# Layer 2 of a graph network: gathered rows in buffers of four, run rows stored in pairs side by side

## Chip, cores and metric

One core of one Trainium2 chip. The time is device microseconds of one execution; the kernel before was run three times.

## What is computed

Four graph layers (mean, max-pool, gcn, mean) over 6250 nodes and 100,000 edges, sorted by destination, and a last product. The change is in the aggregation of layer 2, a maximum over the incoming edges:

```python
def _sage_pool(h, src, dst, n, deg, W_pool, b_pool, W_self, W_neigh, b):
    hp = jax.nn.relu(h @ W_pool + b_pool)
    hmax = jax.ops.segment_max(hp[src], dst, num_segments=n)
    hmax = jnp.where(deg[:, None] > 0, hmax, 0.0)
    return h @ W_self + hmax @ W_neigh + b
```

`hp` has 6250 rows of 512 float32, 2 KB each.

## The kernel before

Everything runs in one program; a framework turns the Python below into instruction streams per engine, orders them, and adds semaphore waits where tiles depend on each other. A tile of a pool with `bufs=n` takes the place of the one made n tiles earlier and waits for its last readers; a pool opened on the memory of a closed one waits for the last readers there.

**Layer 1** gathers rows of `tab_h` (L483), sums them with matrix products and writes `hp` to `tab_p`, the first part of the DRAM tensor `rows2` (L1162). Beside it `segments()` (L596) finds for each edge whether it has the same destination as the one before it in its lane (`same`), and row numbers for a later fix (`fixI`).

**Layer 2's maximum** (L1566 to L1633) works on the edges in six blocks of `BLOCKS = (52, 100, 220, 180, 130, 100)` steps, last block first. In a block of `tb` steps, lane p of the 128 partitions holds `tb` consecutive edges, and step t takes the t-th edge of every lane: one indirect DMA on GpSimd gathers 128 rows of `tab_p` into `X` (L1574), and VectorE folds them into `run`, the maximum since the current destination began (`step`, L1555). Since a node's maximum stands where its last edge was, the running rows must be kept in DRAM, but only one for each pair of steps: the row after the odd step t is made so that it also holds what ended at t-1 (L1589). So each pair has two operations on `run` and one on `X[:, 0, :]`, and one store of that row to the block's part of `rows2`:

```python
        def stored(b, r0, rows):
            n = rows.shape[1]
            nc.sync.dma_start(
                runs[b][r0 * P : (r0 + n) * P, :].rearrange("(g p) f -> p g f", p=P), rows)
```

`X` holds two steps; its six buffers alternate between two pools, `xpool` (three buffers, also scratch memory in layer 1) and `xmore` (three). Row g of lane p lies at `g * P + p` of the block's rows. The last pair of a block stores both rows of `X` at once.

Around the steps, generators are advanced step by step: `products2` (L1326) multiplies the weights together on TensorE and forms the bias rows, and ends with adds to `qrow` (L288, L1352); at step 64 (`MADE_AT`) what is left of it is issued and its pool `fw2` is closed, and the pool `early3` opened on its memory. `finding` (`node_rows`, L1179) computes for every block and node the row in `rows2` that holds its maximum; its first seven pieces come before the steps, the others one every 12 steps from step 130. `build_narrow` makes adjacency tiles with one-hot operands (`hm`, L374). After a block, `carry` (L1358) passes maxima from lane to lane, gathers one row for each lane (`fixf`, L1383) and stores the mended ones; then `done2` (L1459) gathers for each tile of 128 nodes a row from each block it lies in (`tot`, L1450), takes their maximum, multiplies, and writes `tab_r`, which layer 3 gathers. `early_products` begins layer 3's products. All gathers are issued by GpSimd in the order of its stream; stores of `X` are issued by SyncE.

Of the kernel before, what the change touches and what calls it, by code (L numbers as in the profile page):

```python
# [20 lines left out]
P = 128  # L21
# [56 lines left out]
def fast_path(  # L78
# [90 lines left out]


    assert all(tb % 2 == 0 for tb in BLOCKS)
    kept = [tb // 2 + 1 for tb in BLOCKS]

    n_of = [n * P + 1 + P for n in kept]
    run_at = [NP + sum(n_of[b + 1 :]) for b in range(NB)]
# [397 lines left out]
    G2 = 2  # L573
    upto2 = ctx.enter_context(ExitStack())
    ahead = upto2.enter_context(tc.tile_pool(name="ahead", bufs=1, side="right"))
    xpool = upto2.enter_context(tc.tile_pool(name="xrows", bufs=3, side="right"))
    srcI = ahead.tile([P, T], I32, name="srcIf")
    same = ahead.tile([P, T], F32, name="samef")
    fixI = ahead.tile([P, NB], I32, name="fixIf")
# [8 lines left out]
    def kept_row(b, t, whole, half):  # L588

        nc.vector.tensor_copy(whole, t)  # L590
        nc.vector.tensor_single_scalar(whole, whole, 1, op=ALU.logical_shift_right)
        nc.vector.tensor_copy(half, whole)
        nc.vector.tensor_scalar(t, t, -(BLOCKS[b] / 2.0 - 1.0), None, op0=ALU.add)
        nc.vector.tensor_tensor(t, t, half, op=ALU.max)

    def segments():  # L596
        dstI, dstF, eqf = scratch(T, I32), scratch(T), scratch(T)
        flen, fhalf = (ahead.tile([P, 1], F32, name=n) for n in ("flenf", "fhalf"))
        flenI = ahead.tile([P, 1], I32, name="flenI")
        for b, tb in enumerate(BLOCKS):  # L600
            t0 = offs[b] // P
            for flat, put in ((sflat, srcI), (dflat, dstI)):
                tc.keep_in_program_order(nc.sync.dma_start(
                    put[:, t0 : t0 + tb],
                    flat[offs[b] : offs[b + 1]].rearrange("(p t) -> p t", t=tb),
                ))
        for _ in range(60):
            yield 1
        nc.vector.tensor_copy(dstF, dstI)
        nc.vector.tensor_tensor(same[:, 1:], dstF[:, 1:], dstF[:, : T - 1], op=ALU.is_equal)  # L610
        yield 1
        for b, tb in enumerate(BLOCKS):
            t0 = offs[b] // P
            sl_ = slice(t0, t0 + tb)
            nc.vector.memset(same[:, t0 : t0 + 1], 0.0)
            nc.vector.tensor_copy(rows_df[:, b : b + 1], dstF[:, t0 : t0 + 1])
            nc.vector.tensor_copy(rows_dl[:, b : b + 1], dstF[:, t0 + tb - 1 : t0 + tb])
            nc.vector.tensor_scalar(eqf[:, sl_], dstF[:, sl_], rows_df[:, b : b + 1], None,
                                    op0=ALU.is_equal)
            nc.vector.tensor_reduce(flen, eqf[:, sl_], AX.X, ALU.add)  # L620
            nc.vector.tensor_scalar(flen, flen, -1.0, None, op0=ALU.add)
            kept_row(b, flen, flenI, fhalf)
            nc.vector.tensor_scalar(flen, flen, float(P), float(run_at[b]), op0=ALU.mult,
                                    op1=ALU.add)
            nc.vector.tensor_add(fixI[:, b : b + 1], flen, pidx)
            yield 1


# [455 lines left out]
    with ExitStack() as on:  # L1084
# [86 lines left out]
        for d in range(H1):  # L1171
# [2 lines left out]
        sums(wk, psg, tab_h, FI, srcT, keyT, JC * P, H1, done1, 14, hub, counts=3, todo=todo, rest=24,  # L1174
             aside=[own_ahead(), tail_checks(wk), segments()])
    layer1.close()


    def node_rows(pool, psm):  # L1179
# [28 lines left out]
        for b, tb in reversed(list(enumerate(BLOCKS))):  # L1208
            z = float(run_at[b] + kept[b] * P)
            nc.vector.tensor_scalar(q, end, float(offs[b + 1]), -1.0 - offs[b], op0=ALU.min,  # L1210
                                    op1=ALU.add)
            nc.vector.scalar_tensor_tensor(ok, q, 0.0, has, op0=ALU.is_ge, op1=ALU.mult)
            nc.vector.scalar_tensor_tensor(ok, beg, float(offs[b + 1]), ok, op0=ALU.is_lt,
                                           op1=ALU.mult)
            nc.vector.tensor_mul(q, q, ok)
            yield
            nc.vector.tensor_scalar(pI, q, 1.0 / tb, None, op0=ALU.mult)
            nc.vector.tensor_copy(pF, pI)
            nc.vector.scalar_tensor_tensor(t_, pF, -float(tb), q, op0=ALU.mult, op1=ALU.add)
            nc.vector.tensor_scalar(off, t_, 0.0, None, op0=ALU.is_lt)  # L1220
            nc.vector.tensor_sub(pF, pF, off)
            nc.vector.scalar_tensor_tensor(t_, off, float(tb), t_, op0=ALU.mult, op1=ALU.add)
            yield
            nc.vector.tensor_scalar(off, t_, float(tb), None, op0=ALU.is_ge)
            nc.vector.tensor_add(pF, pF, off)
            nc.vector.scalar_tensor_tensor(t_, off, -float(tb), t_, op0=ALU.mult, op1=ALU.add)
            yield
            kept_row(b, t_, pI, off)
            nc.vector.scalar_tensor_tensor(t_, t_, float(P), pF, op0=ALU.mult, op1=ALU.add)

            yield
            nc.vector.scalar_tensor_tensor(off, pF, float(tb), beg, op0=ALU.mult,
                                           op1=ALU.subtract)
            nc.vector.tensor_scalar(off, off, -float(offs[b]), None, op0=ALU.is_ge)
            if b:
                nc.vector.tensor_scalar(pF, pF, float(kept[b] * P + 1), None, op0=ALU.add)
                nc.vector.tensor_sub(pF, pF, t_)
                nc.vector.tensor_mul(pF, pF, off)
                nc.vector.tensor_add(t_, t_, pF)
            else:  # L1240
                nc.vector.tensor_mul(off, off, ok)
                nc.vector.tensor_scalar(pF, pF, 1.0, None, op0=ALU.add)
                nc.vector.tensor_mul(pF, pF, off)
                nc.vector.tensor_scalar(pF, pF, -1.0, None, op0=ALU.add)
                for d in last_tiles:
                    lanes = bank(psm, "pm", "lanes", (P,))
                    nc.tensor.transpose(lanes, pF[:, d : d + 1].to_broadcast([P, P]), ident)
                    yield
                    takes[d] = pool.tile([P, P], F32, name=f"takes{d}", bufs=1)
                    nc.vector.tensor_scalar(takes[d], lanes, pidx, None, op0=ALU.is_equal)  # L1250
            yield
            nc.vector.tensor_scalar(t_, t_, float(run_at[b]), None, op0=ALU.add)
            nc.vector.tensor_sub(off, only, t_)
            nc.vector.tensor_mul(off, off, lone)
            nc.vector.tensor_add(t_, t_, off)
            nc.vector.tensor_scalar(t_, t_, -z, None, op0=ALU.add)
            nc.vector.tensor_mul(t_, t_, ok)
            nc.vector.tensor_scalar(rows_of[b], t_, z, None, op0=ALU.add)
            yield
# [31 lines left out]
    with tc.tile_pool(name="fl2c", bufs=1) as ck, ExitStack() as late:  # L1291
# [11 lines left out]
        nc.scalar.dma_start(mkR, stash_k[:, 1, RB1:])  # L1303
        keepT = ck.tile([P, NB, P], F32, name="keepTf")
        contT = ck.tile([P, NB, P], F32, name="contTf")
        xmore = late.enter_context(tc.tile_pool(name="xrows2", bufs=3))

        def chains():

# [244 lines left out]
        def step(put, held, st, row):  # L1554
            nc.vector.scalar_tensor_tensor(put, held, st, row, op0=ALU.mult, op1=ALU.max)  # L1555

        def stored(b, r0, rows):
            n = rows.shape[1]
            nc.sync.dma_start(
                runs[b][r0 * P : (r0 + n) * P, :].rearrange("(g p) f -> p g f", p=P), rows)  # L1560

        tiles, begun2, begun_at = [], 0, 0
        ends = []
# [2 lines left out]
        for b in reversed(range(NB)):  # L1566
            tb = BLOCKS[b]
            t0 = offs[b] // P
            run = psr.tile([P, FH], F32, name="run")
            for s0 in range(0, tb, G2):  # L1570
                X = (xmore if at // G2 % 2 else xpool).tile([P, G2, FH], F32, name="X2")
                for k in range(G2):
                    t = t0 + s0 + k
                    nc.gpsimd.indirect_dma_start(  # L1574
                        out=X[:, k, :], out_offset=None, in_=tab_p,
                        in_offset=bass.IndirectOffsetOnAxis(ap=srcI[:, t : t + 1], axis=0),
                    )
                    row, st = X[:, k, :], same[:, t : t + 1]
                    if s0 + G2 >= tb:
                        step(row, X[:, 0, :] if k else run, st, row)  # L1580
                        if k:
                            stored(b, s0 // 2, X)
                    elif k == 0 and s0:
                        step(run, run, st, row)
                    elif k:
                        held = run if s0 else X[:, 0, :]
                        if s0 == 0:
                            step(run, held, st, row)
                        step(X[:, 0, :], row, st, held)  # L1589
                        if s0:  # L1590
                            step(run, run, st, row)
                        stored(b, s0 // 2, X[:, :1, :])
                    at += 1
                    if at > 8:
                        next(steps, None)
# [4 lines left out]
                    if at == MADE_AT:  # L1600
                        for _ in steps:
                            pass
                        top.close()
                        early_pool.append(
                            top.enter_context(tc.tile_pool(name="early3", bufs=1)))
                    if at <= EARLY_AT:
                        hub.advance(math.ceil(len(first) * max(0, at - 16) / (EARLY_AT - 16)))
                    else:
# [18 lines left out]
                    for g in list(now):  # L1627
                        if next(g, 0) == 0:
                            now.remove(g)
            end = carry(b, X[:, 1, :])  # L1630
            next(end)
            ends.append(end)
            last_b = b  # L1633
# [784 lines left out]
```

## Time and profile before

| | |
|---|---|
| median of 3 runs | 2730.45 us (2728.73 to 2737.01) |
| the profiled execution | 2726.43 us |
| its span on the core | 2724.6 us |
| granted TensorE clock, mean | 0.944 |
| busy shares of the span | PE 87%, VectorE 76%, GpSimd 71%, ScalarE 33% |
| DMA | 805.91 MB, mean 296 GB/s |
| gathers of X (L1574) | 782, 742.5 us busy |
| steps on VectorE (L1555) into run, into X | 758, 571.0 us; 379, 281.4 us |
| stores of X (SyncE) | 385 of 256 KB, 6 of 512 KB |

The profile shows one execution. A group's line gives its source line, engine and operation, the tiles written and read, the count, the busy time and mean duration, and the idle time of the engine just before, with what ended it. A row of stretches gives start and end, length, busy time with count for each engine, then the granted clock, the mean share in which the 16 DMA engines were busy, and GB/s. A row of the timeline gives start, length, engine, line and operation, and in brackets the idle time before it and its releaser. A row of the chain gives start, length and what the chain that ended last went through.

### The profile page before, as it was taken

How to read it: one execution, taken by the hardware profiler on the slowest of the kernel's cores; microseconds unless marked ns; L12 is line 12 of the kernel's file. 1: busy time of each engine (PE TensorE's matmuls, PEld its weight loads, DVE VectorE, ACT ScalarE, POOL GpSimd, SP SyncE). 2: the span in 40 equal slices, each digit the busy share in tenths (PEclk: the TensorE clock that was granted, in tenths of full speed). 3: DMA queues.
4: the chain of work that ended last, by engine and by line, in shares of the span. 5: the costliest groups of instructions: out<-in, count | busy, mean ns of one | idle time of the engine just before them, and what ended most of it. 6: DMA issues, size and time to landing. Idle time of an engine off the chain costs nothing.

```text
span 2724.6 us, 39212 instructions
## 1 busy us (share of the span) xinstructions
PE 2368.6 (87%) x11542; PEld 1282.5 (47%) x11674; DVE 2076.7 (76%) x5555; ACT 904.5 (33%) x2190; POOL 1938.3 (71%) x2266
## 2 busy tenths in 40 slices
PE   4698999999786675989899939986999999999998
PEld 2356667677443332434344414442444444565554
DVE  8898777766699798889789988972767766466665
ACT  5567767764388777212111111110000101000000
POOL 6477777777577777777677777745777775677776
PEclk8799999999897887999899969998999999999999
DMA  9467677777799999999999999979999998888886
GB/s 288 150 185 206 206 211 216 217 230 221 245 377 354 337 362 362 345 359 352 312 351 356 348 336 344 348 243 351 379 378 393 386 363 309 248 239 240 238 247 200
DMA packets 352251, 805.91 MB, mean 296 GB/s; under 512 B 56174, under 2 KB 150870, under 8 KB 351996
## 3 DMA queue, kind: packets, MB, share of 16 engines
q0 software_dynamic: 146080, 513.79, 57.3%
q1 hardware_dynamic: 139368, 206.78, 20.9%
q10 hardware_dynamic: 66580, 82.73, 8.9%
q8 instruction: 95, 1.56, 0.2%
q14 instruction: 128, 1.05, 0.1%
HBM read 604.99 MB, written 198.91 MB: 295 GB/s over the span
## 4 chain that ended last, share of the span: by engine, by line
PE 47%; DMA 28%; DVE 12%; issue 6%; POOL 3%; ACT 1%; ACTq 0%; SPq 0%; DVEq 0%; another core or an unknown queue 0%; POOLq 0%
PE pd L564 12%; PE pg L505 11%; DMA X<-rows,srcIf 11%; DVE run L1555 5%; PE pd L556 4%; DMA rows<-X 4%; DMA ring<-tab_h,srcT 4%; PE pm_hp L1157 3%; DVE X L1555 3%; DMA ring<-tab_s,srcE 2%; PE pd L557 2%; POOL X L1574 2%; PE pm_hp L1154 2%; PE pb L346 2%; PE pg L500 2%
## 5 line engine op out<-in xcount | busy, mean ns | idle before, releaser
L1574 POOL DMA_INDIRECT X<-rows,srcIf x782 | 742.5, 950 | 276.3 <-issue 146.4
L1555 DVE SCALAR_TENSOR_TENSOR run<-run,samef,X 128x512 f32<-128x512 f32 x758 | 571.0, 753 | 42.3 <-DMA X<-rows,srcIf 37.1
L483 POOL DMA_INDIRECT ring<-tab_h,srcT x474 | 456.3, 963 | 148.9 <-issue 56.4
L505 PE MATMUL pg<-ring,hot 128*128 128x259 bf16 (+1 forms) x2432 | 512.1, 320 | 53.2 <-DMA ring<-tab_h,srcT 30.7
L534 DVE SCALAR_TENSOR_TENSOR acc<-pg,M,acc 128x256 f32<-128x256 f32 (+2 forms) x694 | 356.3, 538 | 106.0 <-PE pg L505 76.8
L483 POOL DMA_INDIRECT ring<-tab_r,srcE x342 | 331.7, 970 | 133.5 <-issue 54.9
L564 PE MATMUL pd<-r,ae 128*128 128x512 bf16 x1492 | 372.6, 385 | 32.9 <-DVE acc L1286 30.3
L483 POOL DMA_INDIRECT ring<-tab_s,srcE x314 | 299.4, 954 | 117.5 <-PE pg L501 38.6
L505 PEld LDWEIGHTS <-hot 128*128 128x128 bf16 x2448 | 239.6, 98 | 257.8 <-issue 98.3
L1555 DVE SCALAR_TENSOR_TENSOR X<-X,samef,run 128x512 f32<-128x512 f32 x379 | 281.4, 742 | 43.0 <-DMA X<-rows,srcIf 13.1
L556 PE MATMUL pd<-zt,ac 128*128 128x512 bf16 x835 | 291.0, 382 | 7.1 <-DMA ac<-tab_a 5.5
L564 PEld LDWEIGHTS <-ae 128*128 128x128 fp8e4 x1536 | 151.6, 99 | 250.3 <-issue 110.1
L479 DVE TENSOR_SCALAR hot<-iota_bf,keyE 128x128 bf16<-128x128 bf16 x656 | 159.3, 267 | 115.1 <-PE pg L505 82.0
L557 PE MATMUL pd<-zt,ac 128*128 128x256 bf16 x882 | 241.6, 274 | 2.7 <-DVE zt L312 0.2
L564 PE MATMUL pd<-zt,ac 128*128 128x512 bf16 x797 | 221.8, 380 | 0.9
L1482 PE MATMUL pm_prf<-unf,hTf 128*128 128x512 f32 x384 | 187.8, 615 | 5.6 <-ACT hTf L1472 5.4
L564 PE MATMUL pd<-Z,A 128*128 128x256 bf16 (+1 forms) x1176 | 184.4, 274 | 0.7 <-ACT A L351 0.6
L338 ACT ACTIVATE hs<-ht,onef 128x128 bf16<-128x128 bf16 x396 | 153.4, 393 | 90.2 <-PE pb L346 88.6
L346 PE MATMUL pb<-hm,hs 128*128 128x392 bf16 x461 | 146.3, 337 | 11.7 <-DVE hm L340 11.5
L337 ACT ACTIVATE ht<-iota_bf,sk 128x128 bf16<-128x128 bf16 x396 | 153.0, 398 | 8.3
L340 DVE TENSOR_SCALAR hm<-iota_w,mk 128x392 bf16<-128x392 f16 x461 | 149.7, 332 | 5.2 <-PE pb L346 4.7
L479 DVE TENSOR_SCALAR hot<-iota_bf,keyT 128x128 bf16<-128x128 bf16 x474 | 122.5, 267 | 40.6 <-PE pg L505 39.4
(381 smaller groups left out, 3498.9 us busy)
## 6 DMA issues: line engine op xcount, KB each, us to landing
rows<-X SPq DMA_DIRECT2D x385, 256.0 KB
tab_r<-r ACTq DMA_DIRECT2D x49, 384.0 KB
rows<-hpf SPq DMA_DIRECT2D x49, 256.0 KB
th<-tab_t ACTq DMA_DIRECT2D x49, 256.0 KB
X<-rows,srcIf POOLq DMA_INDIRECT x782
ac<-tab_a ACTq DMA_DIRECT2D x90, 112.0 KB
tab_t<-th SPq DMA_DIRECT2D x37, 256.0 KB
tab_h<-Z SPq DMA_DIRECT2D x16, 579.0 KB
```

What stands on the lines that cost most here:

```text
L338: nc.scalar.activation(hots[0], t, AF.Relu, bias=one, scale=-1.0)
L346: nc.tensor.matmul(hold[0], hots[0], hots[1], start=(k == 0), stop=(k == k_of[w] - 1))
L479: nc.vector.tensor_scalar(hot[j], iota_b, keyT[:, j - jb : j - jb + 1], None, op0=ALU.is_equal)
L483: nc.gpsimd.indirect_dma_start(out=ring[:, j % deep, :], out_offset=None, in_=table, in_offset=bass.IndirectOffsetOnAxis(ap=srcT[:, j - jb ...
L505: nc.tensor.matmul(pg[:, : F + c], hot[j], X[:, part * F : (part + 1) * F + c], start=(k == 0 and part == 2), stop=(k == n - 1 and part == 1),
L534: nc.vector.scalar_tensor_tensor(acc[d], half, m, acc[d], op0=ALU.mult, op1=ALU.add)
L556: nc.tensor.matmul(hold[0], a, z[:, : 2 * F], start=(s == ss[0]), stop=False)
L557: nc.tensor.matmul(hold[0][:, :F], a, z[:, 2 * F :], start=False, stop=(s == ss[-1]))
L564: nc.tensor.matmul(hold[0][:, : F + c], a, z[:, part * F : (part + 1) * F + c], start=(s == ss[0] and part == 2 and s != own), stop=(s == ...
L1482: nc.tensor.matmul(pm, hT[:, c, :], un[:, c, :], start=False, stop=(c == KH - 1))
L1555: nc.vector.scalar_tensor_tensor(put, held, st, row, op0=ALU.mult, op1=ALU.max)
L1574: nc.gpsimd.indirect_dma_start(out=X[:, k, :], out_offset=None, in_=tab_p, in_offset=bass.IndirectOffsetOnAxis(ap=srcI[:, t : t + 1], axis=0),
```

## The change

`X` now holds four steps. Its buffers come in turn from `xrows2` (two) and `xrows3` (one), and from step 64 on also from `xrows4` (one), which is opened after `early3` on the memory that `fw2` left. The run row of the first pair goes to `X[:, 0, :]`, that of the second to `X[:, 1, :]`, and both leave in one store after the fourth step. In DRAM the two lie side by side for each lane: row g of lane p is at `(g // 2) * 2 * P + 2 * p + g % 2`, and `kept` rounds the rows of a block up to even. `twin` turns a row g into `g + (g // 2) * (2 * P - 2)` for the row numbers in `segments` and `node_rows`. The last buffer of a block is stored whole, two or four rows. `xpool` is closed after layer 1.

```diff
-    kept = [tb // 2 + 1 for tb in BLOCKS]
+    kept = [(tb // 2 + 2) // 2 * 2 for tb in BLOCKS]
...
+    def twin(t, whole, half):
+
+        nc.vector.tensor_copy(whole, t)
+        nc.vector.tensor_single_scalar(whole, whole, 1, op=ALU.logical_shift_right)
+        nc.vector.tensor_copy(half, whole)
+        nc.vector.scalar_tensor_tensor(t, half, float(2 * P - 2), t, op0=ALU.mult, op1=ALU.add)
...
             kept_row(b, flen, flenI, fhalf)
-            nc.vector.tensor_scalar(flen, flen, float(P), float(run_at[b]), op0=ALU.mult,
-                                    op1=ALU.add)
-            nc.vector.tensor_add(fixI[:, b : b + 1], flen, pidx)
+            twin(flen, flenI, fhalf)
+            nc.vector.tensor_scalar(flen, flen, float(run_at[b]), None, op0=ALU.add)
+            nc.vector.scalar_tensor_tensor(fixI[:, b : b + 1], pidx, 2.0, flen, op0=ALU.mult,
+                                           op1=ALU.add)
...
             kept_row(b, t_, pI, off)
-            nc.vector.scalar_tensor_tensor(t_, t_, float(P), pF, op0=ALU.mult, op1=ALU.add)
+            twin(t_, pI, off)
+            nc.vector.scalar_tensor_tensor(t_, pF, 2.0, t_, op0=ALU.mult, op1=ALU.add)
...
-        xmore = late.enter_context(tc.tile_pool(name="xrows2", bufs=3))
+        xpools = [upto2.enter_context(tc.tile_pool(name="xrows2", bufs=2, side="right")),
+                  late.enter_context(tc.tile_pool(name="xrows3", bufs=1))]
+        xpools.append(xpools[0])
...
-        def stored(b, r0, rows):
+        def stored(b, h, rows):
             n = rows.shape[1]
             nc.sync.dma_start(
-                runs[b][r0 * P : (r0 + n) * P, :].rearrange("(g p) f -> p g f", p=P), rows)
+                runs[b][2 * h * P : (2 * h + n) * P, :].rearrange("(g p t) f -> p g (t f)", p=P, t=2),
+                rows.rearrange("p (g t) f -> p g (t f)", t=2))
...
-            for s0 in range(0, tb, G2):
-                X = (xmore if at // G2 % 2 else xpool).tile([P, G2, FH], F32, name="X2")
-                for k in range(G2):
+            for s0 in range(0, tb, 4):
+                n = min(4, tb - s0)
+                X = xpools[0].tile([P, 4, FH], F32, name="X4")
+                xpools.append(xpools.pop(0))
+                for k in range(n):
...
-                    if s0 + G2 >= tb:
-                        step(row, X[:, 0, :] if k else run, st, row)
-                        if k:
-                            stored(b, s0 // 2, X)
-                    elif k == 0 and s0:
+                    put = X[:, k // 2, :]
+                    if s0 + k >= tb - 2:
+                        if k % 2 == 0:
+                            step(put, run, st, row)
+                        else:
+                            last = X[:, k // 2 + 1, :]
+                            step(last, put, st, row)
+                            stored(b, s0 // 4, X[:, :n, :])
+                    elif k % 2 == 0 and s0 + k:
                         step(run, run, st, row)
-                    elif k:
-                        held = run if s0 else X[:, 0, :]
-                        if s0 == 0:
+                    elif k % 2:
+                        held = run if s0 + k > 1 else X[:, 0, :]
+                        if s0 + k == 1:
                             step(run, held, st, row)
-                        step(X[:, 0, :], row, st, held)
-                        if s0:
+                        step(put, row, st, held)
+                        if s0 + k > 1:
                             step(run, run, st, row)
-                        stored(b, s0 // 2, X[:, :1, :])
+                        if k == 3:
+                            stored(b, s0 // 4, X[:, :2, :])
...
                         early_pool.append(
                             top.enter_context(tc.tile_pool(name="early3", bufs=1)))
+                        xpools.append(top.enter_context(tc.tile_pool(name="xrows4", bufs=1)))
```

More of the change, by code (lines that the diff above doesn't have):

```diff
@@ L575, in fast_path @@
     ahead = upto2.enter_context(tc.tile_pool(name="ahead", bufs=1, side="right"))
-    xpool = upto2.enter_context(tc.tile_pool(name="xrows", bufs=3, side="right"))
+    upto1 = ctx.enter_context(ExitStack())
+    xpool = upto1.enter_context(tc.tile_pool(name="xrows", bufs=3, side="right"))
     srcI = ahead.tile([P, T], I32, name="srcIf")
@@ L1176, in fast_path @@
     layer1.close()
+    upto1.close()
     def node_rows(pool, psm):
@@ L1629, in fast_path @@
                             now.remove(g)
-            end = carry(b, X[:, 1, :])
+            end = carry(b, last)
             next(end)
```

## Prediction

> **What bounds the kernel now.** The change touches layer 2 alone, so I read that stage first by stretches, then GpSimd's order of time in it, then its groups, the DMA queues and the chain. Layer 2 runs from the first gather (721 us) to the last store (1824 us):
>
> ```profile
> core 0: us, PE busy (x) PEld busy (x) DVE busy (x) ACT busy (x) POOL busy (x), PEclk, DMA share, GB/s
> 721.00:1824.00 1103.00, 904.79 (x3259) 429.82 (x3305) 975.97 (x1904) 412.43 (x897) 800.24 (x844) 0.90 0.98 346
> ```
>
> The tempting reading is the DMA share of 0.98: the stage looks bound by its transfers, which this change makes cheaper. GpSimd looks idle for a quarter of the stage. Its timeline says otherwise:
>
> ```profile
> 842.51 0.95 POOL L1574 DMA_INDIRECT X<-rows,srcIf  x1 [0.30 <-issue]
> 843.76 0.95 POOL L1574 DMA_INDIRECT X<-rows,srcIf  x1 [0.30 <-issue]
> 845.01 0.95 POOL L1574 DMA_INDIRECT X<-rows,srcIf  x1 [0.30 <-DMA rows<-X]
> 846.26 0.95 POOL L1574 DMA_INDIRECT X<-rows,srcIf  x1 [0.30 <-issue]
> ```
>
> Gathers start every 1.25 us: 0.95 busy and 0.30 that no wait explains, the same 0.30 whether a releaser is named or not. Is that period GpSimd's own, or does a full DMA hold it back? The gathers of layer 1 (first row below) answer: 462 in 586 us is 1.27 each at a DMA share of 0.71. So 1.25 us is GpSimd's own cost of an indirect DMA.
>
> ```profile
> 104.00:690.00 586.00, 444.98 (x462) 0.98 0.71 209
> 721.40:821.80 100.40, 72.13 (x76) 0.92 0.99 362
> 821.80:842.40 20.60, 15.12 (x16) 1.00 1.02 388
> 842.40:865.10 22.70, 15.38 (x16) 0.82 0.97 323
> 865.10:1815.30 950.20, 639.05 (x674) 0.90 0.98 345
> ```
>
> ```profile
> L1574 POOL DMA_INDIRECT X<-rows,srcIf x782 | 742.5, 950 | 276.3 <-issue 146.4 <-DVE run L1555 35.5 <-DVE X L1555 25.6
> L1450 POOL DMA_INDIRECT tot<-rows,rows_of x55 | 52.0, 946 | 16.8 <-issue 10.4 <-DMA rows<-X 2.1 <-DMA X<-rows,srcIf 1.5
> L1383 POOL DMA_INDIRECT fixf<-rows,fixIf x5 | 4.7, 944 | 1.5 <-issue 0.9 <-DVE cTf L1373 0.3 <-DVE segf L1369 0.3
> L1555 DVE SCALAR_TENSOR_TENSOR X<-X,samef,run 128x512 f32<-128x512 f32 x379 | 281.4, 742 | 43.0 <-DMA X<-rows,srcIf 13.1 <-issue 12.9 <-DVE hm L374 7.0
> ```
>
> 843 indirect DMAs (782, 55, 5 and one more total) by 1.25 are 1054 us of the 1094 from 721.4 to 1815.3. All real waiting of GpSimd is the other 40: 6 in the first 92 steps (121.0 less 115), 2.7 in the next 16, and 31.5 behind (950.2 less 735 by 1.25). The number of gathers doesn't change. So the change can win at most these waits, and every microsecond by which it holds GpSimd back is never caught up.
>
> **The change part by part.**
>
> *Fewer, larger stores.* The built program has 196 stores of X instead of 391, nearly all with 4 KB side by side per lane.
>
> ```profile
> q0 software_dynamic: 67440, 221.04, 58.9%
> q1 hardware_dynamic: 75952, 113.28, 27.7%
> q10 hardware_dynamic: 21504, 46.32, 11.3%
> rows<-X SPq DMA_DIRECT2D x385, 256.0 KB
> ```
>
> q1 carries them: 27.7% of 1103 us is 306 us for 113 MB, 2.7 us a MB at 1.5 KB a packet; q10 pays 2.7 at 2.2 KB, so packet size matters little. Between nothing and 5% of the stores' 104 MB gives 0 to 14 us of 16-engine time. GpSimd paces the stage, so I take 0 on the path, bounds -14 and 0. SyncE loses 195 issues it had time for: 0. The Trainium skill, "DMA: Bandwidth & Descriptors", section "Rules for kernel authors", says to coalesce many small transfers into one large one; by it this part gains, and it is a rival below. The same page, section "Anatomy of one DMA", has a DMA cost about 2.0 us plus its bytes at 436 GB/s, an estimate of 0.6 us later landing for 512 KB than for 256 KB, which speaks against it where someone waits for the landing.
>
> *Three buffers of four, until step 64.* A buffer is filled again when its store has landed. The chain prices gathers and stores under load:
>
> ```profile
> 783.77 6.28 DMA X<-rows,srcIf
> 790.90 5.88 DMA rows<-X
> 860.62 5.50 DMA rows<-X
> 870.15 5.10 DMA X<-rows,srcIf
> ```
>
> So a gather takes about 5.7 us until its step can run, a store 5.7 until GpSimd goes on. Before, a buffer's round is 1.25 (two issues) + 5.7 + 1.1 (DVE for the last row) + 5.7 = 13.8 us (the 1.1 is the 0.74 of its operation, L1555 above, and some waiting), and six buffers of two give GpSimd 12 by 1.25 = 15.0: 1.2 to spare. Now the fourth issue comes 3.75 after the first: 16.3 us against the same 15.0. The ring binds: 15 us for the first 12 steps and 64 by 1.36 for the rest of the first 76 are 102 us, beside 100.4 measured. If all the early hiccups (about 5) add to that and stores land 0.7 later (5 rounds, 4 us), it is +11; if they vanish in the ring, +2. I take +6.
>
> *The fourth buffer.* xrows4 is opened after step 64 on the memory of fw2, the pool of the weight products. I read the built order and its waits: the first gather into it (steps 76 to 79) waits for the last reader there, the add of b4r to qrow, and GpSimd gets the gathers of steps 80 to 91 ahead of it. DVE has no step to do between step 75 and that gather. In its order there now stand 145 instructions between step 75's last and the add of qrow: 13 hm, three adds of the bias rows, and 129 small ones, the row numbers of node_rows pulled forward.
>
> ```profile
> 847.27 3.60 PE L282 MATMUL pm_b<-B4f,col 128*128 128x512 f32 x8
> 851.77 0.60 DVE qrowf L288
> 852.55 0.33 DVE qrowf L1352
> 827.99 0.75 DVE L1555 SCALAR_TENSOR_TENSOR run<-run,samef,X 128x512 f32<-128x512 f32 x1
> 736.94 0.18 DVE L1224 TENSOR_SCALAR nr<-nr 128x49 f32<-128x49 f32 x1
> 737.21 0.20 DVE L1225 TENSOR_TENSOR nr<-nr,nr 128x49 f32<-128x49 f32 x1
> 737.33 0.20 DVE L1226 SCALAR_TENSOR_TENSOR nr<-nr,nr 128x49 f32<-128x49 f32 x1
> L374 DVE TENSOR_SCALAR hm<-iota_w,mkR 128x196 bf16<-128x196 f16 x320 | 87.5, 284 | 0.9 <-PE pb L390 0.8
> ```
>
> The 827.99 row is step 75's last operation, ending 828.7; with the +6 it ends at 834.7. Small operations follow each other at 0.27 us where one needs the last (736.94 to 737.21), 0.12 where not. At 0.20 they take 26 us (15 to 35), hm 3.7, the adds 1.8: the add of qrow ends at 866 (855 to 875). TensorE's products put it at 853 at the earliest, as now. So the gather of step 76 starts at 866, where it started at 821.8. Queued behind it on GpSimd is every later gather, the carries' and totals' too; DVE waits for its rows.
>
> Steps 92 to 95 need that same buffer once more: 3.75 + 5.7 + 1.1 + 5.5 = 16 after 866, so 882, where before they began at 842.4: **+40 us** (+27 if qrow is at 853).
>
> *Afterwards, four buffers.* 16 rows give 20 us against a round of 16.3: 3.7 to spare, where there were 1.2. A hiccup of DVE that costs GpSimd something now costs up to 2.5 less, and the row numbers are already out of DVE's way. Of the 31.5 us of later waiting I give back 11; bounds 4 (they come in clusters at the ends of blocks, where one allowance serves several) and 25.
>
> *Row numbers, twin.* A net of four tiny DVE operations a block in layer 1 and in node_rows: hidden, since GpSimd paces layer 1 too; the second lot is in the 145. 0, up to 3 if uncovered.
>
> *Last store.* The last four rows of a block go out in one store, 1 MB instead of 512 KB, two of its four rows unused or raw. At the end, the last totals wait for it:
>
> ```profile
> 1823.56 0.37 SPq L1559 DMA_DIRECT2D rows<-X  x1
> 1827.28 0.94 POOL L1403 DMA_INDIRECT tot<-rows,rows_of  x1 [11.13 <-DMA rows<-X]
> ```
>
> 512 KB more at 346 GB/s: +1.
>
> **Sum.** +40 - 11 + 1 = +30 us on the profiled execution's 2726.4 (its span of 2724.6 and 1.8 around it): 2756.4. The median of the runs, 2730.45, lies 4.0 above that execution, so **2760**, 1.1% slower. The 2726.4 is the fastest seen; runs reached 2737.
>
> **Rivals.**
> - *DVE is early* (0.17): the row numbers run at the short spacing and the gather waits for TensorE's products alone, 853. Then +27, less some 14 as the ring relaxes, +1: 2744. For it: nothing but the spacing; against: most row-number operations need the one before.
> - *No recovery* (0.10): 875 for qrow and only 4 given back: +49 - 4 + 1, some 2776. It decides if the hiccups come from TensorE's accumulations, which no longer ring helps.
> - *All recovered* (0.08): 853, and 25 of the 31.5 back: +3, 2734, not to be told from no change.
> - *Faster* (0.05): the other side. If the DMA engines are the bound after all, at 0.98, the 14 us of cheaper packets come off the stage, and the fourth buffer's stall is filled from rows gathered ahead: 2716. It decides if gathers come closer than 1.25 us once the engines are less full. Against it stands layer 1, with the same period at 0.71.
> - That the change doesn't do what it says is excluded by the built program: stores of 128 by 1024 elements and 16 rows in rotation are there.
>
> **How the numbers follow.** The forecast has 0.60. The range reaches from a little under the early-DVE case's 2744 (for a better recovery) to just over the no-recovery case: 2737 to 2778; outside lie the faster case, the all-recovered one and the tails, some 0.18. 0.3% is 8 us, about what a measurement of this kernel can tell from no change. Slower: 0.60 + 0.17 + 0.10 = 0.87; same 0.08; faster 0.05.
>
> **What would show it.** Right: the gather period still 1.25 us; GpSimd with one wait of about 20 us before the gather of step 76 (it is through with step 91 near 847: 842.4 + 6 less one period) and one of about 11 before step 92; DVE doing a block of nr operations near 835 to 866 with no step between; the stage's DMA share lower there; step 108's gather some 40 us later than 865; q1's share of the stage a little down. Wrong: no such gap around 850, or a period under 1.25, or waits of GpSimd in the later 950 us that grow instead of shrinking; then the stage's length is set by something that I put beside the path.

## The result and the profile after

The changed kernel takes 2771.54 us (median of 5 runs, 2766.84 to 2775.26); the kernel before, run beside it, 2734.47 us (5 runs, 2728.73 to 2737.01). The ratio is 1.0139 (95% interval 1.0121 to 1.0158): slower by 37 us, against 30 forecast, inside the range. The profiled execution took 2773.45 us, its span 2771.6.

The stretches of layer 2 again, cut at the same gathers as in the prediction (length, GpSimd busy with its count, granted clock, DMA share, GB/s). The first is layer 1; the next four are the first 76 gathers, 16, 16, and then the 734 later ones in two pieces:

```profile
104.00:690.00 586.00, 442.45 (x460) 0.98 0.73 208
726.70:838.60 111.90, 72.34 (x76) 0.94 0.97 337
838.60:888.60 50.00, 15.54 (x16) 0.71 0.49 162
888.60:910.40 21.80, 15.52 (x16) 0.50 0.86 274
910.40:1100.90 190.50, 135.20 (x142) 0.74 0.96 343
1100.90:1855.40 754.50, 561.93 (x592) 0.93 0.97 348
```

The last two rows of the kernel before, cut in the same way:

```profile
865.10:1047.60 182.50, 135.19 (x142) 0.77 0.99 352
1047.60:1815.20 767.60, 561.47 (x592) 0.93 0.98 343
```

Length against length: +11.5 for the first 76 gathers (111.9 to 100.4), +29.4 for the next 16 (50.0 to 20.6), -0.9, then +8.0 and -13.1. GpSimd's timeline after shows the two gaps that the prediction named; it issues steps 80 to 91 first, so the row at 874.21 is the gather of step 76 and the one at 888.66 that of step 92:

```profile
853.47 0.95 POOL L1590 DMA_INDIRECT X<-rows,srcIf  x1 [0.30 <-issue]
854.72 0.95 POOL L1590 DMA_INDIRECT X<-rows,srcIf  x1 [0.30 <-issue]
874.21 0.94 POOL L1590 DMA_INDIRECT X<-rows,srcIf  x1 [18.55 <-PE pb L390]
875.46 0.94 POOL L1590 DMA_INDIRECT X<-rows,srcIf  x1 [0.30 <-issue]
876.71 0.95 POOL L1590 DMA_INDIRECT X<-rows,srcIf  x1 [0.30 <-issue]
877.96 0.95 POOL L1590 DMA_INDIRECT X<-rows,srcIf  x1 [0.30 <-issue]
888.66 0.94 POOL L1590 DMA_INDIRECT X<-rows,srcIf  x1 [9.75 <-DVE hm L374]
```

The named releasers, an accumulation and an `hm`, are only what ended last nearby: `pb` and `hm` do not touch the buffer or its memory. What the first gather waits for is seen in the list of the tile `qrowf` (duration min/median/max, start), and in what VectorE does between its last step and that add (a stretch, its operations on `nr` alone):

```profile
L284 ACT COPY qrowf<-pm_b x1: 587/587/587, 854.5 to 854.5; 128x512 f32<-128x512 f32 x1
L288 DVE TENSOR_TENSOR qrowf<-qrowf,b2rf x1: 684/684/684, 872.2 to 872.2; 128x512 f32<-128x512 f32 x1
L1365 DVE TENSOR_TENSOR qrowf<-qrowf,b4rf x1: 417/417/417, 873.0 to 873.0; 128x256 f32<-128x256 f32 x1
```

```profile
845.40:872.20 26.80, 21.56 (x127) 0.77 0.33 101
```

TensorE and ScalarE were through at 855; VectorE's two adds came at 872.2 to 873.4, behind 26.8 us of other work, in the main these 127 small operations. The gather follows 0.8 us later.

The stores of layer 2 (packets, MB, share of the stretch; the sizes of the issues) are half as many and twice as large, and q1's share fell from 27.7% to 25.9% of a stretch that is 42 us longer:

```profile
q1 hardware_dynamic: 48016, 115.10, 25.9%
rows<-X SPq DMA_DIRECT2D x191, 512.0 KB
rows<-X SPq DMA_DIRECT2D x5, 1024.0 KB
```

### The profile page after: what moved, and what is told of

The parts are those of the page before. It is cut to its first block, busy times and chain, and to the rows that moved or that the text cites. A ratio compares the mean times of both kernels' runs of the same rounds, so it can differ in the third digit from the quotient of the medians.

```text
span 2771.6 us, 38669 instructions
## 1 busy us (share of the span) xinstructions
PE 2361.2 (85%) x11542; PEld 1279.0 (46%) x11674; DVE 2091.4 (75%) x5603; ACT 906.7 (33%) x2190; POOL 1940.3 (70%) x2266
## 4 chain that ended last, share of the span: by engine, by line
PE 55%; DMA 26%; DVE 10%; issue 4%; POOL 4%; ACT 1%; ACTq 0%; SPq 0%; DVEq 0%; POOLq 0%
PE pd L564 16%; PE pg L505 11%; DMA X<-rows,srcIf 11%; PE pd L556 5%; DMA ring<-tab_h,srcT 4%; PE pm_prf L1495 3%; DVE run L1568 3%; PE pm_hp L1166 3%; PE pd L557 3%; POOL X L1590 3%; PE pm_hp L1163 2%; DMA ring<-tab_s,srcE 2%; PE pm_prf L1489 2%; PE pg L500 2%; PE pb L346 2%
## 5 line engine op out<-in xcount | busy, mean ns | idle before, releaser
L505 PEld LDWEIGHTS <-hot 128*128 128x128 bf16 x2448 | 238.6, 98 | 264.6 <-issue 102.3
```

The costliest lines, as they stand in the source:

```text
L505: nc.tensor.matmul(pg[:, : F + c], hot[j], X[:, part * F : (part + 1) * F + c], start=(k == 0 and part == 2), stop=(k == n - 1 and part == 1),
```

## The experiments

Each time stands beside the kernel before on the same chip, and each ratio is to that. The stretches under a run are cut at the same gathers: 76, 16, 16, 142 and 592 of them.

**The fourth buffer later** (from the changed kernel):

```diff
+        fourth = []
...
-                        xpools.append(top.enter_context(tc.tile_pool(name="xrows4", bufs=1)))
+                        fourth.append(top.enter_context(tc.tile_pool(name="xrows4", bufs=1)))
+                    if at == 112:
+                        xpools.append(fourth.pop())
```

> As the changed kernel, but the fourth buffer joins the rotation at step 112 instead of 64, when the weight products are long through. If the loss is the wait for the fourth buffer's memory (18.2 us before step 76's gather and 9.5 before step 92's in the changed kernel's trace, and what the held-up start cost), it goes: three buffers of four for 48 more steps cost some 0.1 us a step, 5 us, so 2771.5 - 40 + 5 = about 2736 us, and no gap of GpSimd over 8 us between 830 and 900 us. If the loss lies in the coarser buffers and the later landing of a store of 512 KB, it stays at 2765 us or more, since those are kept and the three-buffer stretch is longer.

Measured: 2740.64 us beside 2735.69, ratio 1.0018 (1.0007 to 1.0030). The stretch of 50.0 is 22.0, and no gap of GpSimd there is over 5 us:

```profile
721.40:836.10 114.70, 72.24 (x76) 0.93 0.96 332
836.10:858.10 22.00, 15.16 (x16) 0.89 0.87 293
858.10:878.80 20.70, 15.79 (x16) 0.50 0.93 308
878.80:1071.20 192.40, 135.21 (x143) 0.77 0.96 339
1071.20:1828.20 757.00, 561.92 (x593) 0.93 0.98 348
```

Each beside its own kernel before, the changed kernel is 37 us slower and this one 5, so the join at step 64 is worth 32 us of the 37. The rival, coarse buffers alone, falls as the main cause; but they do cost something, since the first row, 114.7, and the fourth, 192.4, stay as long as in the changed kernel.

**One store a pair** (from the changed kernel, with `stored1` writing one row into its place):

```diff
...
-                        if k == 3:
-                            stored(b, s0 // 4, X[:, :2, :])
+                        stored1(b, s0 // 2 + k // 2, put)
```

> As the changed kernel, but each pair's run row is stored by itself as soon as it is made: 256 KB, 2 KB a lane with 4 KB between lanes, the same rows in the same places. If a cheaper transfer is worth nothing on the path (GpSimd issues a gather every 1.25 us whatever the DMA engines carry), the time is that of the changed kernel within 6 us (2766 to 2777), with a period of 1.25. If larger stores help and the DMA engines bound the stage, up to 14 us are lost again: 2780 to 2786. If the later landing of the large store is what costs, the time drops by some 5 rounds of 0.7 us early and as much later: about 2764.

Measured: 2767.10 us, ratio 1.0113 (1.0093 to 1.0133), within the first expectation and near the third; its interval overlaps the changed kernel's. The queue of the stores in its layer 2, and its first, second and fourth stretch:

```profile
q1 hardware_dynamic: 76085, 116.43, 27.4%
```

```profile
723.00:832.10 109.10, 72.01 (x76) 0.91 0.98 343
832.10:878.40 46.30, 15.56 (x16) 0.79 0.54 182
...
900.80:1094.10 193.30, 135.72 (x143) 0.72 0.97 338
```

With 58% more packets in that queue the stage is not longer. The first 76 gathers take 2.8 us less than with the large stores, but the changed kernel and the run above, which do the same up to there, differ as much (111.9 and 114.7). The larger store brings nothing here; that it costs anything by landing later was not told apart from nothing.

The Trainium skill's advice to coalesce many small transfers ("DMA: Bandwidth & Descriptors", "Rules for kernel authors") gained no time in this stage; the row calls transfers under 64 KB mostly overhead, and the stores were of 256 KB already. The same page of the Trainium skill gives the 2.0 us and 436 GB/s that the prediction quotes for DMAs issued by GpSimd, while these stores are issued by SyncE; no run here shows their landing by itself.

**The order of rows alone** (from the kernel before: `kept`, `twin`, and each row stored to its new place):

```diff
...
+                at_b = runs[b][r // 2 * 2 * P : (r // 2 + 1) * 2 * P, :]
+                nc.sync.dma_start(at_b.rearrange("(p t) f -> p t f", t=2)[:, r % 2, :],
+                                  rows[:, i, :])
```

> The kernel before with only the order of the rows in DRAM and the row numbers changed: buffers of two, one store a pair, as before. If the row numbers cost nothing (my term: 0, at most 3), the time is 2734 within 5 us, and the first gather of layer 2 starts near 721 us. If the changed kernel's later start of layer 2 (726.7 against 721.4) comes from the added row-number operations, it starts near 727 here too and the time is about 2739. The other cause would be run-to-run variation or the changed pools.

Measured: 2741.41 us beside 2735.69, ratio 1.0018 (1.0006 to 1.0029): 2 to 8 us, more than the 0 that I took. They are not the row numbers' alone: the edit also splits the last store of each block and writes a spare row in five of them (402 stores of 256 KB, where there were 385 and 6 of twice the size). Layer 2 starts at 720.7 here, so nothing shows that the added operations of layer 1 made the changed kernel start at 726.7. But the profiled execution, 2734.62, is the fastest of the twelve and no longer than the kernel before, so it cannot show where the 5 us arise.

**Two more buffers of two, late** (from the kernel before):

```diff
+                        fourth = top.enter_context(tc.tile_pool(name="xrows4", bufs=2))
...
+                turn = (xpool, xmore)
+                if at >= 112:
+                    turn = (xpool, fourth, xmore, xpool, xmore, fourth, xpool, xmore)
```

> The kernel before, with two more buffers of two from step 112 on the memory that the weight products left: 16 rows in rotation as in the changed kernel, in finer buffers, without the early stretch of three coarse ones. GpSimd waits for some 31 us behind step 108 in the kernel before. If a longer ring gives back 4 to 25 of these (I took 11), the time is 2734.5 - 11 = 2723 us (2709 to 2730). If those waits come from VectorE's and TensorE's own order, the ring gives back nothing and the time stays at 2734 within 4.

Measured: 2719.99 us beside 2735.69, ratio 0.9940 (0.9919 to 0.9961), 15.7 us faster. The last two stretches:

```profile
863.50:1041.60 178.10, 134.78 (x143) 0.80 1.00 360
1041.60:1798.60 757.00, 562.43 (x593) 0.93 0.98 348
```

Behind the first 250 gathers the 16 rows in pairs are as fast as the 16 in fours (757.0 here and in the run with the fourth buffer later). The difference lies ahead of them: 102.3 against 114.7 in the first 76 gathers, where the one kernel has six pairs and the other three fours, and 178.1 against 192.4 in the 142.

**Three buffers of four to the end** (the line of `xrows4` left out of the changed kernel):

> As the changed kernel without the fourth buffer: three buffers of four to the end. By my round of a buffer (16.3 us against 15.0 for the 12 gathers that the ring lets ahead) each step costs 1.36 us instead of 1.25, 0.11 for 770 steps, so 2735.7 + 85 = about 2820 us, with no long wait around step 76. If the round is shorter than I reckoned and three buffers do, 2740 to 2750 us, which would make the fourth buffer a pure loss.

Measured: 2805.32 us beside 2734.39, ratio 1.0262 (1.0239 to 1.0286): +71, where I reckoned 85. The whole length is slower, no single wait:

```profile
882.00:1083.50 201.50, 134.90 (x143) 0.76 0.93 318
1083.50:1899.70 816.20, 560.19 (x593) 0.92 0.94 324
```

**Two more buffers of two from step 64, and from step 88** (the run from 112 with another number):

```diff
-                if at >= 112:
+                if at >= 64:
```

> The kernel before with two more buffers of two, as in the run that had them from step 112, but from step 64, as the changed kernel joins its fourth. If the loss is the wait for memory that the add of qrow still reads (129 row-number operations stand ahead of that add in VectorE's built order here too), one long wait of GpSimd stands near 840 to 880 us and the time is 2720 + 25 to 40, 2745 to 2760 us. If the long wait belongs to buffers of four, it is absent and the time is 2712 to 2722.

> The same from step 88. The first gather into the new memory is that of step 90 or so, at 840 us, and TensorE's products let the add of qrow end at 853 at the earliest; part of the row-number operations stand ahead of it. By the wait theory: a wait of 10 to 25 us and 2730 to 2745 us, between the runs from 112 and from 64. If joining early is harmless, 2715 to 2720.

Measured: 2751.45 us, ratio 1.0077 (1.0057 to 1.0096), from 64; 2727.05 us, ratio 0.9973 (0.9960 to 0.9987), from 88. GpSimd's timeline and the last add to `qrowf` of the run from 64, then of that from 88:

```profile
821.76 0.94 POOL L1577 DMA_INDIRECT X<-rows,srcIf  x1 [0.30 <-issue]
853.26 0.94 POOL L1577 DMA_INDIRECT X<-rows,srcIf  x1 [30.55 <-PE pb L390]
...
865.02 0.94 POOL L1577 DMA_INDIRECT X<-rows,srcIf  x1 [7.06 <-DVE hm L374]
L1352 DVE TENSOR_TENSOR qrowf<-qrowf,b4rf x1: 420/420/420, 852.0 to 852.0; 128x256 f32<-128x256 f32 x1
```

```profile
862.39 1.01 POOL L1577 DMA_INDIRECT X<-rows,srcIf  x1 [3.08 <-PE pb L390]
...
873.85 0.94 POOL L1577 DMA_INDIRECT X<-rows,srcIf  x1 [6.70 <-DVE hm L374]
L1352 DVE TENSOR_TENSOR qrowf<-qrowf,b4rf x1: 418/418/418, 861.2 to 861.2; 128x256 f32<-128x256 f32 x1
```

The wait is there with buffers of two as well; it belongs to the memory. In both runs the gather starts 0.8 us after the add's end, as in the changed kernel. From 88 the two waits, 3.1 and 6.7 us, come to just under the 10 to 25 that I expected, and the time to just under 2730: joined 24 steps later, the new buffers were first asked for near the time at which the add was done.

**The row numbers first** (from the changed kernel):

```diff
-        for _ in range(7):
-            next(finding)
+        for _ in finding:
+            pass
```

> As the changed kernel, but all pieces of the row numbers (node_rows) are issued ahead of the steps, so that VectorE does them among its first steps and the add of qrow stands right behind the last step before it. If the 129 operations ahead of the add hold the fourth buffer back, the wait of 18.2 us before step 76's gather shrinks by 5 to 13 us (TensorE's products end at 853 at the earliest), while the first 76 steps may lose some of it as VectorE has more to do there: 2755 to 2768 us. If the order on VectorE did not matter and TensorE alone set that wait, it stays at 18 us and the time at 2771 or more.

Measured: 2833.50 us beside 2734.39, ratio 1.0378 (1.0357 to 1.0398), 62 us above the changed kernel. Neither expectation had it: the time is one that the second allows, but the wait is not the 18 us of the second, it is 96. TensorE's waits from 722 to 846 us (total, times, longest), then the tile `qrowf` and GpSimd's wait:

```profile
PE pb L390 <- DVE hm L374: 70.6, 50, 6.2
```

```profile
L284 ACT COPY qrowf<-pm_b x1: 586/586/586, 950.3 to 950.3; 128x512 f32<-128x512 f32 x1
L1365 DVE TENSOR_TENSOR qrowf<-qrowf,b4rf x1: 419/419/419, 951.8 to 951.8; 128x256 f32<-128x256 f32 x1
953.01 0.94 POOL L1590 DMA_INDIRECT X<-rows,srcIf  x1 [96.01 <-PE pb L390]
```

The numbers did leave the place ahead of the add, which now follows ScalarE's copy by 1.5 us instead of 18.5. But VectorE, full with steps and numbers, made the one-hot operands late; the accumulations `pb` that need them waited 71 us, and the weight products queued behind them on TensorE ended near 950 instead of 855. The fourth buffer waited for the same add, 79 us later. As a forecast of what the new order would do it is a miss; for the cause it agrees. In four kernels (the changed one, the two joins from 64 and 88, and this one) the gather starts 0.8 us after that add's end, while it starts 2 to 19 us after the end of ScalarE's copy: the gather waits for the add, whichever engine makes it late.

**Buffers of one row** (from the kernel before: for the even steps seven, held until the store has landed, for the odd steps five; in the second kernel nine and seven from step 112):

```diff
...
+        turn = [[(xeven, "XE", 6)] * 6 + [(xmore, "XE", 1)], [(xmore, "XO", 5)] * 5]
...
+                    if at == 112:
+                        turn[0] += [(fourth, "XE", 2)] * 2
+                        turn[1] += [(fourth, "XO", 2)] * 2
```

> The kernel before with buffers of one row: seven for the even steps of a pair (held until the store of the run row has landed) and five for the odd steps (free as soon as VectorE has read them), 12 rows of memory as before, from the first step. By the round arithmetic an even row's buffer has 7 by 2.5 = 17.5 us for its round of 13.8 and an odd one 12.5 for 5.7 + 1.1 and some waiting: 3.7 us to spare instead of 1.2, as the ring of 16 rows in fours was reckoned, without any join. If the ring's slack is what the waits hang on, 8 to 16 us go: 2719 to 2727. If they hang on VectorE's lag at the ends of blocks alone, the time stays at 2735 within 4.

> The same, and from step 112 two more buffers for the even and two for the odd steps on the memory that the weight products left: 8.7 us to spare. If slack goes on paying, GpSimd's waits behind step 108 all but vanish and the time is 2706 to 2716, the best of all. If the run with eight buffers of two had already taken all that a ring can give, it is 2720 within 4.

Measured: 3264.51 us, ratio 0.9964 (0.9935 to 0.9994), and 3276.91 us, ratio 1.0000 (0.9976 to 1.0024), on a chip where the kernel before took 3280.66. Layer 2 of the first of them, from its first gather of `X` to its last, has 843 indirect DMAs in 1354.6 us (one per 1.61) at 280 GB/s:

```profile
856.10:2210.70 1354.60, 802.37 (x843) 0.84 0.86 280
```

These absolute times stand beside no other run's. So both ran again:

> The kernel with seven even and five odd buffers of one row once more: the chip of its first run took some 3280 us for the kernel before too, with DMA transfers that left GpSimd waiting in layer 1 as well. On a chip that takes about 2735 us for the kernel before, the question of that run stands: 2719 to 2727 if the ring's slack is what the waits hang on, 2731 to 2739 if not.

> The kernel with nine even and seven odd buffers of one row from step 112 once more, for the same reason: 2706 to 2716 us if slack goes on paying, 2716 to 2724 if the run with eight buffers of two had taken all that a ring can give.

Measured: 2734.16 us beside 2733.55, ratio 0.9999 (0.9983 to 1.0014), with 12 rows; 2718.93 us, ratio 0.9946 (0.9927 to 0.9966), with 16. The last two stretches with 12 rows, then with 16:

```profile
866.00:1052.50 186.50, 136.22 (x142) 0.77 0.98 348
1052.50:1821.20 768.70, 560.80 (x592) 0.93 0.98 342
```

```profile
863.70:1046.10 182.40, 135.72 (x142) 0.79 0.99 356
1046.10:1798.70 752.60, 560.42 (x593) 0.93 0.99 349
```

By my arithmetic of rounds, 12 rows in single buffers have as much to spare (3.7 us) as 16 in fours. They bring nothing; 16 rows bring 15 us in pairs and in singles alike. On the chips of some 2735 us, in the last stretch all kernels with 16 rows take 752 to 757 us, whether in fours, pairs or singles, and those with 12 in pairs or singles 767.6 to 769.5. So there the waits hang on how many rows GpSimd may be ahead of VectorE, not on the spare time of a buffer's round as I reckoned it.

## Why the prediction was right, step by step

Four kernels make a square: pairs or fours, with the 16 rows from step 64 or from 112.

| us (less the kernel before beside it) | from 112 | from 64 |
|---|---|---|
| 16 rows in pairs | 2719.99 (-15.7) | 2751.45 (+17.1) |
| 16 rows in fours, stored together | 2740.64 (+5.0) | 2771.54 (+37.1) |

In the differences it is 21 and 20 us down, 33 and 32 across. So from the kernel before: longer ring -16, fours with their order of rows and their stores +21, early join +32. That the three add up to the 37 follows from the table; what the square shows is that the early join costs the same with pairs and fours, and fours the same with either join.

- **GpSimd's 1.25 us as the bound: held.** Where a timeline above shows no wait, gathers come every 1.25 us, also from 874 to 878 in the stretch with a DMA share of 0.49, and layer 1 has 460 in 586 us at 0.73. The rival *Faster* is refuted: gathers do not come closer when fewer packets are sent, and splitting the stores again cost nothing. No run took load off the transfers without also changing the ring.
- **The fourth buffer, +40 by step 92: held, its two parts shifted.** VectorE's last step ahead of the join ended at 845.4, 16.7 later than before (828.7): 5.3 from a later start of layer 2, 11.4 from the ring of three fours, where the term was +6 and its upper bound 11 (the two other profiled kernels with the same three fours take 113.2 and 114.7 for the 76 gathers, so it was too small). From there to the gather of step 76 it took 28.8 us, where I had 31.3 (834.7 to 866): 127 operations on `nr`, one per 0.21 us with what stands between them, as sized. From step 76's gather to step 92's it took 14.5, against 16. Step 92's gather moved from 842.4 to 888.7, or 40.9 counted from the first gather. The rival *DVE is early* had the add at 853; ScalarE's copy was there at 855, and VectorE was not.
- **The longer ring, -11: the mis-sized term.** Stretch by stretch the changed kernel lost 8.0 us in the 142 gathers behind step 108 and then won 13.1 back. The loss goes with buffers of four, though not with them alone: 190.5, 192.4 and 193.3 us in three kernels with 16 rows in fours, and 178.1 to 182.4 in the pairs from 112 and from 64 and in the singles with 16. (The 193.3 is the kernel with one store a pair, so it isn't the large store.) In the changed kernel two waits make it up:

```profile
1034.81 0.95 POOL L1590 DMA_INDIRECT X<-rows,srcIf  x1 [0.30 <-issue]
1042.14 0.94 POOL L1590 DMA_INDIRECT X<-rows,srcIf  x1 [6.38 <-DVE run L1568]
1087.92 1.00 POOL L1590 DMA_INDIRECT X<-rows,srcIf  x1 [6.07 <-DMA rows<-X]
```

  Here VectorE lagged, and a buffer of four comes free only after its fourth step and its store. The kernel with the row numbers first has 16 rows in fours too, and its 142 gathers take no longer than those of the pairs. VectorE had 97 `hm` to make there instead of 126 (26.8 us instead of 34.6), since more of them were made during GpSimd's long wait; that this is why it lost nothing fits, but was not shown.

```profile
987.30:1167.10 179.80, 135.22 (x142) 0.72 0.98 360
```

  I had given fours and pairs the same worth for the same spare time. Of the gain a part is not one: GpSimd runs further ahead at the end and then waits longer for the last store (15.67 against 11.13 us before the last `tot`). Measured at VectorE's last step, the rows below (kernel before, then after), it moved from 1823.5 to 1867.2, +38.3 from the first gather, so 40.9 and 2.6 back, where 11 stood (one execution each; the medians lie 10 us closer together than these two, so the 2.6 is rough):

```profile
1822.78 0.75 DVE L1555 SCALAR_TENSOR_TENSOR X<-X,samef 128x512 f32<-128x512 f32 x1
```

```profile
1866.40 0.75 DVE L1568 SCALAR_TENSOR_TENSOR X<-X,samef 128x512 f32<-128x512 f32 x1
1872.06 0.94 POOL L1416 DMA_INDIRECT tot<-rows,rows_of  x1 [15.67 <-DMA rows<-X]
1873.64 2.07 PE L1431 MATMUL pc_last<-fixf,takes 128*128 128x512 f32 x2 [0.68 <-ACT fixf L1393]
```

- **The last store, +1: right in size, but not on the path.** 512 KB at 346 GB/s are rather 1.5; from the last step's end to the last `tot` it is 4.9 us against 3.7. The carry's products (`pc_last`) start 6.5 us after that step's end in both kernels (1873.6 after, 1830.0 before), later than the `tot` gather, and in both the chain that ended last goes through VectorE's `acc`, `fixf` and `pc_last`, not through `tot`.
- **Row numbers, 0 with at most 3: probably too low.** The run with the order of rows alone lost 2 to 8 us, with 11 more stores than the kernel before; which of the two costs it, and where, stays open.
- **The sum.** The profiled executions differ by 47.0: start of layer 2 +5.3, layer 2 to VectorE's last step +38.3, the rest +3.4. The first and the last were not forecast. The start of layer 2 lay at 719.0 to 721.7 in four executions whose code up to there is that of the kernel before, at 720.7 to 726.7 in the six with the changed row numbers, and at 724.0 in one with 16 single rows, which has none of them; so I count it as variation, without having shown it. The profiled execution of before, 2726.43, was also shorter than all five runs beside it. The medians' 37 is the better number. The forecast of 30 was 7 short of it: fours and row numbers too cheap by 14 (6 + 1 + 0 against 21), the longer ring's gain too small by 5 (16 with pairs; in the changed kernel the fours take most of it back), the early join near its size (34 of the 40, against 32). That these errors partly cancel, and the time came out so near, is luck; the wait itself was rightly foreseen in place, cause and size.

The fastest kernel here has the late join and no fours: 2718.93 and 2719.99 us, 0.5% to 0.6% below the kernel before.

## What to carry to other kernels

A buffer opened on memory that a closed pool leaves is not free when the pool closes, but when the last reader there has run in its engine's order; take it into the rotation only then, or everything queued behind its first use waits. Where one engine issues at a fixed period, count how many items it may be ahead of the consumer and how coarsely they come free: 16 rows from step 112 on gained 16 us in pairs, and the kernel with fours throughout lost 5. Moving work out of one engine's queue can push another engine's last product further back, so read the new order before expecting a gain.

## What the runs showed of the hardware that I had not expected

One chip ran the kernel before in 3280.66 us, 20% longer than the others. In the profile of the kernel with 12 single rows there, GpSimd's gathers still took 0.95 us each, but came one per 1.61 us in layer 2, at 280 GB/s, where the kernel before has 346 elsewhere. So on that chip the period of 1.25 us was not what bounded layer 2. There the extra rows were worth nothing (1.0000, 0.9976 to 1.0024), where they were worth 0.5% elsewhere; why that chip's transfers were slower stays open.
